# A conditional linear layer and a mixture of experts on one core: weight masks by halves on two engines, one bank for counts and ranks, an uneven last store

## The chip, the cores and the metric

The kernel runs on one core of a Trainium2 chip. The metric is device time in microseconds (us), the median of several runs; a run counts from the start of the program's execution on the core to its end. A profile is one execution of its own, with a time of its own. In it, PE is TensorE's matmuls and PEld its weight loads, DVE is VectorE, ACT is ScalarE, POOL is GpSimd, SP is SyncE. A name with a q behind it (SPq, ACTq) is that engine's queue, from which it issues transfers.

## The reference

Two layers with residuals over x of 128 batch rows x 32 tokens x 128 features, in float32. The first builds a weight matrix for every batch row from eight masked ones; the second routes every batch row to two of eight experts and adds a shared MLP.

```python
masked_w = weight * mask[None, :, :]                  # (8, 128, 128)
w_bot = einsum('bg,got->bot', cond_8, masked_w)
x = x + einsum('bnt,bot->bno', x, w_bot) + bias
...
rw = softmax(cond_8); w, sel = top_k(rw, 2)            # per batch row
w = w / w.sum(-1)                                     # and a scaling that keeps the value
out = sum over experts of dense_w[:, e] * mlp_e(x)    # gelu(x gate_e) * (x up_e), times down_e
x = x + out + mlp_shared(x)                           # all MLPs 128 -> 512 -> 128
```

## The kernel before, in words

Everything is held transposed: features on 128 partitions, the 4096 tokens along the free axis, in eight tiles of 512 (NTILE = 8, TB = 512; one tile holds 16 batch rows). The order of instructions on each engine is the order of the program text. It has three parts.

**Conditional layer, woven with the routing.** The eight weights arrive as four transfers of 128 KB, in turns on SP and ACT (L88 to L94); the mask follows the first on SP, then come two tiles of x, the bias, the shared MLP and the other six tiles. POOL makes the identity `ident` and the constant `ones` (L124 to L126). `warm_up(n)` (L130) issues n matmuls of ones by ones on PE, whose result nobody reads: four first, and six behind the transpose of the conditions, `ps_y` (L227). One float32 matmul is two records, here called passes; a transpose is one.

DVE then forms `mw`, weight times mask (L233 to L239), in four operations of two weights each, and after them `yd` (L241), which spreads `ps_y` over the eight weights. `transpose_weights` (L250) turns `mw` by eight transposes on PE, two to a bank; ACT and DVE copy the four banks in turns to `wT`. At its end it takes three steps of the routing.

`make_weights(i, half)` (L275) is one unit: 16 matmuls of 32 rows (32 passes) into four banks, which give 64 of the 128 outputs for 32 batch rows, in the order: block k outside, bank j inside. Then ACT copies banks 0 and 2 to `W`, DVE banks 1 and 3. There are eight units, 0 to 7; units 2i and 2i+1 belong to pair i of tiles. `apply_weights(t)` (L301) multiplies x by W into a bank `pz`, ACT copies it to `z`; `finish_cond(t)` (L320) transposes z back into a bank `pt`, DVE adds bias and x to give `x1`, and for tiles from 2 on POOL copies x1 to `acc`. The loop at L677 to L693 runs three units, and then, for pair i, two apply_weights, `advance(4)`, two units while there are any, and two finish_cond.

PSUM has eight banks in three pools: three g, three u, two o. `bank()` (L268) takes them by the cycle "guoguogu". A bank is taken when it is first written, and is free again after its last reader.

`routing()` (L353) is a generator. A `yield` ends a step of one to three small operations on DVE; `advance(n)` takes up to n steps, after it has issued the matmuls that earlier steps left behind (`tensor_later`). `yield ROUND` ends an advance. Step 5 asks for two matmuls: `ps_n`, how many rows each expert has, into a g bank, and `ps_p`, each row's rank in its expert, into a u bank (L372 to L375). They run at the start of the advance in pair 1. `count` (L403, step 10) reads ps_n, `slot` and `over` (L461 and L465) read ps_p.

**Experts.** Each tile gathers up to six batch rows of one expert (192 tokens): SP loads the three weights, POOL copies the rows, `Mlp` runs the matmuls, DVE adds the weighted result to `acc`. Two shared tiles run ahead of them.

**Late shared tiles.** Tiles 2 to 7 of the shared MLP. `Mlp.hidden` makes 512 columns of one of four hidden blocks (gate and up on PE, gelu on ACT, product `h` on DVE), `Mlp.down` multiplies it into `ps_out`. A `Pipeline` keeps `lag` blocks between the two. The last tile has `parts=2` (L725): its output is summed in two banks of 256 columns, first columns 0 to 255 and then the rest for every block; `finish` (L609) adds acc to each and stores the first from SP, the second from ACT.

Of the kernel before, what the change touches and what calls it, by code (L numbers as in the profile page):

```python
# [10 lines left out]
F32 = mybir.dt.float32  # L11
# [3 lines left out]
ALU = mybir.AluOpType  # L15
# [7 lines left out]
S = 6  # L23
S2 = 4
# [6 lines left out]
def kernel(  # L31
# [37 lines left out]
    const = ctx.enter_context(tc.tile_pool(name="const", bufs=1))  # L69
    small = ctx.enter_context(tc.tile_pool(name="small", bufs=1))  # L70
# [14 lines left out]
    cond_sb = const.tile([B, G], F32, name="cond_sb")  # L85
    nc.scalar.dma_start(out=cond_sb, in_=cond)
    mask_sb = const.tile([P, P], F32, name="mask_sb")
    GQ = 2  # L88
    w0_sb = []
    for q in range(G // GQ):  # L90
        wq = const.tile([P, GQ, P], F32, name=f"w0_{q}", tag=f"w0_{q}")
        engine = nc.scalar if q % 2 else nc.sync
        engine.dma_start(out=wq, in_=w0T[:, ts(q, GQ), :])
        w0_sb.append(wq)  # L94
        if q == 0:
            nc.sync.dma_start(out=mask_sb, in_=maskT)
    x_sb = []

    def load_x(t):
# [18 lines left out]
    shared = load_mlp(const, sgate, sup, sdown, "s")  # L118
    for t in range(EARLY, NTILE):
        load_x(t)  # L120


    ident = const.tile([P, P], F32, name="ident")
    make_identity(nc, ident)  # L124
    ones = const.tile([P, P], F32, name="ones")
    nc.gpsimd.memset(ones, 1.0)  # L126

    warm = ps_u.tile([P, TB], F32, name="warm", tag="u")

    def warm_up(n):  # L130
        for _ in range(n):
            nc.tensor.matmul(warm[:, 0:P], ones, ones, start=True, stop=True)  # L132

    warm_up(4)
    table = small.tile([P, 1], F32, name="table")
    nc.scalar.activation(table, ones[:, 0:1], AF.Exp)

# [3 lines left out]
        out=own,  # L141
        in_=ones[:, 0:R],
# [7 lines left out]
        out=own,  # L150
        in_=own,
# [9 lines left out]
        out=before,  # L161
        in_=ones,
# [30 lines left out]
    before_h = const.tile([P, P], BF16, name="before_h")  # L193
# [15 lines left out]
    own4 = const.tile([P, OQ], F32, name="own4")  # L209
# [16 lines left out]
    ps_y = ps_o.tile([P, TB], F32, name="ps_y", tag="acc")  # L226
    nc.tensor.transpose(  # L227
        ps_y[:, 0:B], cond_rep.rearrange("b r g -> b (r g)"), ident
    )
    warm_up(6)  # L230

    mw = const.tile([P, P, G], F32, name="mw")
    for q in range(G // GQ):  # L233
        nc.vector.tensor_tensor(
            mw[:, :, ts(q, GQ)].rearrange("p o g -> p g o"),
            w0_sb[q],
            mask_sb.unsqueeze(1).to_broadcast([P, GQ, P]),
            ALU.mult,
        )  # L239
    yd = const.tile([P, B, OQ], F32, name="yd")  # L240
    nc.vector.tensor_tensor(  # L241
        yd,
        ps_y[:, 0:B].unsqueeze(2).to_broadcast([P, B, OQ]),
        own4.unsqueeze(1).to_broadcast([P, B, OQ]),
        ALU.mult,
    )
    wT = const.tile([P, NQ, P], F32, name="wT")
    QB = TB // P

    def transpose_weights():  # L250
        TQ = QB // 2
        for i in range(NQ // TQ):
            pool, tag = (ps_u, "u") if i % 2 else (ps_g, "g")
            pt = pool.tile([P, TQ * P], F32, name="pt", tag=tag)
            for k in range(TQ):
                q = i * TQ + k
                nc.tensor.transpose(  # L257
                    pt[:, ts(k, P)],
                    mw[:, ts(q, OB), :].rearrange("p o g -> p (o g)"),
                    ident,  # L260
                )
# [11 lines left out]
    NB = TB // (QB * OQ)  # L273

    def make_weights(i, half):  # L275

# [76 lines left out]
    def routing():  # L353
# [92 lines left out]
        for k, n, i in ((0, NE, 0), (1, NE2, NE)):  # L446
# [12 lines left out]

        slot = small.tile([P, E], F32, name="slot")  # L460
        nc.vector.scalar_tensor_tensor(  # L461
            slot, tile0[:, 0, :], float(S), ps_p[:, 0:E], ALU.mult, ALU.add
        )
        over = small.tile([P, E], F32, name="over")
        nc.vector.scalar_tensor_tensor(  # L465
            over, tiles[:, 0, :], float(S), ps_p[:, 0:E], ALU.mult, ALU.is_le
        )
        yield
        end = small.tile([P, E], F32, name="end")
# [56 lines left out]
    class Mlp:  # L526


        def __init__(self, n, x_in, weights, finish, parts=1):
            self.n, self.x_in, self.finish, self.parts = n, x_in, finish, parts  # L530
# [26 lines left out]
            nc.vector.tensor_tensor(h[:, 0:n], ge[:, 0:n], pu[:, 0:n], ALU.mult)  # L557
            return h

        def down(self, group, h):  # L560
            if self.ps is None:
                self.ps = [
                    ps_o.tile([P, TB], F32, name="ps_out", tag="acc")
                    for _ in range(self.parts)
                ]
            w = self.n // self.parts
            for part, ps in enumerate(self.ps):
                for i, c in enumerate(group):
                    self.product(
                        ps[:, 0:w],  # L570
                        self.wd[:, c, :],
                        h[:, i * self.n + part * w : i * self.n + (part + 1) * w],
                        start=(c == 0),
                        stop=(c == NCH - 1),
                    )
                if group[-1] == NCH - 1:
                    self.finish(ps, part)

    class Pipeline:

# [22 lines left out]

    pipe = Pipeline(h_pool)

    def shared_tile(t, parts=1):
        w = TB // parts

        def finish(ps, part):  # L609
            cols = slice(t * TB + part * w, t * TB + (part + 1) * w)  # L610
            if t < EARLY:
                nc.vector.tensor_tensor(acc[:, cols], ps[:, 0:w], x1[:, cols], ALU.add)
            else:
                o = o_pool.tile([P, w], F32, name="o", tag="o")
                nc.vector.tensor_tensor(o, ps[:, 0:w], acc[:, cols], ALU.add)  # L615
                queue = nc.scalar if part % 2 else nc.sync
                queue.dma_start(out=outT[:, cols], in_=o)

        return Mlp(TB, x1[:, ts(t, TB)], shared, finish, parts)

    def tokens(i, pairs, engine):
        _, values = nc.values_load_multi_w_load_instructions(
# [46 lines left out]
    def weights():  # L669
        unit = units.pop(0)  # L670
        next(unit)
        next(unit)
# [6 lines left out]
    for i in range(LAST + 1):  # L679
        for t in range(PAIR):  # L680
            apply_weights(i * PAIR + t)
        advance(4)

        for _ in units[0:2]:
            weights()
        if i == LAST:
            pipe.run(first, slice(1, 2))
        for t in range(PAIR):
            finish_cond(i * PAIR + t)
        if i == LAST - 1:  # L690
            first = shared_tile(0)
            pipe.run(first, slice(0, 1))
            advance(2)  # L693
# [34 lines left out]

    with tc.If(n_used > SURE, preferred_fallthrough_block=False) as more_tiles:
# [64 lines left out]
```

## Time and profile before

| What | us |
|---|---|
| median of three runs (289.8 to 290.52) | 290.5 |
| the profiled execution, its own time | 289.53 |
| its span, first to last instruction | 287.8 |
| PE busy in the span | 281.1 (98%) |
| DVE busy | 166.6 (58%) |
| ACT busy | 78.9 (27%) |
| POOL busy | 48.4 (17%) |
| landing of the first weights, issued at 0.82 | 2.2 later |
| landing of the mask, issued at 1.26 | 3.0 later |
| the mask products on DVE, four | 4.32 to 6.36 |
| first expert matmul | 50.17 |
| last instruction of an engine (DVE, the last add) | ends at 283.86 |

The busy times are sums over the whole span. In the chain that ended last, each line is a piece: when it began, how long it lasted, and what ran, with x and the number of instructions. In the timeline, each line is a group of like instructions: start, time, engine, line of the code, operation, what it writes and reads with shapes, how many, and in brackets how long the engine had been idle before and for what it had waited. Matmuls overlap in PE's pipeline, so the spacing of their starts tells their cost, not the time of one.

### The profile page before, as it was taken

Reading aid. Unit: us, or ns where it says so; the run is one execution under the profiler, and the core shown is the slowest. Engines: PE = TensorE matmul, PEld = TensorE weight load, DVE = VectorE, ACT = ScalarE, POOL = GpSimd, SP = SyncE. Lnnn points to the kernel's source line nnn. Section 1 sums busy time; section 2 is a strip of 40 time slices with the busy share of each in tenths; the row PEclk is TensorE's granted clock in tenths of the full one; section 3 lists DMA queues with packets and bytes.
Section 4 is the critical chain, followed back from the end, with each engine's and each line's share of the span. In section 5 each row is a group of like instructions: output and inputs, shape, how many; then the busy total and the mean of one; then the engine's idle time right before and its main releaser. Section 6 shows DMA issues by size and latency. Waiting matters only on the chain.

```text
span 287.8 us, 12876 instructions
## 1 busy us (share of the span) xinstructions
PE 281.1 (98%) x5098; PEld 209.0 (73%) x5098; DVE 166.6 (58%) x472; ACT 78.9 (27%) x149; POOL 48.4 (17%) x288
## 2 busy tenths in 40 slices
PE   7999999999999999999999999999999999999993
PEld 7987644687888878878888899999997444444442
DVE  4879783366656666756666666566666333233232
ACT  4655312222222222222222222222222221222220
POOL 3002203122222212222222221312200000000000
PEclk9999999999999999999999999999999999999999
DMA  6800077276658667687667776787710200100001
GB/s 205 281 5 3 0 191 249 77 216 192 204 188 249 205 205 213 198 247 219 197 205 224 211 210 204 206 241 206 218 43 2 74 36 0 39 36 8 28 36 46
DMA packets 41058, 41.86 MB, mean 145 GB/s; under 512 B 2848, under 2 KB 27296, under 8 KB 40992
## 3 DMA queue, kind: packets, MB, share of 16 engines
q1 hardware_dynamic: 40416, 40.58, 46.3%
q8 instruction: 42, 0.69, 1.0%
q10 hardware_dynamic: 576, 0.40, 0.4%
q14 instruction: 24, 0.20, 0.2%
HBM read 38.87 MB, written 2.10 MB: 142 GB/s over the span
## 4 chain that ended last, share of the span: by engine, by line
PE 97%; DVE 1%; POOL 0%; issue 0%; POOLq 0%
PE pg L542 30%; PE ps_out L542 29%; PE pu L542 29%; PE w L282 3%; PE pz L307 3%; PE warm L132 2%; PE pt L324 1%; PE pt L257 0%; DVE o L615 0%; DVE W L296 0%; PE ps_w L347 0%; PE ps_y L227 0%; POOL ident masks.py:199 0%; POOL ident masks.py:197 0%; POOL ones L126 0%
## 5 line engine op out<-in xcount | busy, mean ns | idle before, releaser
L557 DVE TENSOR_TENSOR h<-ge,pu 128x384 f32<-128x384 f32 (+1 forms) x117 | 69.4, 593 | 76.6 <-PE pu L542 74.8
L555 ACT ACTIVATE ge<-pg 128x384 f32<-128x384 f32 (+1 forms) x117 | 61.5, 526 | 189.0 <-PE pg L542 185.5
L655 DVE SCALAR_TENSOR_TENSOR acc<-ps_out,slot_w,acc 128x32 f32 x260 | 65.3, 251 | 30.5 <-DVE h L557 19.5
L542 PE MATMUL pg<-xg,wg 128*32 128x192 f32 (+1 forms) x1440 | 75.7, 320 | 0.0
L542 PE MATMUL ps_out<-h,wd 128*32 128x192 f32 (+1 forms) x1440 | 75.7, 320 | 0.0
L542 PE MATMUL pu<-xg,wu 128*32 128x192 f32 (+1 forms) x1440 | 75.7, 320 | 0.0
L650 POOL COPY xg<-x 128x32 f32 x260 | 42.0, 209 | 132.3 <-PE pu L542 120.1
L542 PEld LDWEIGHTS pg<-xg,wg 128*32 128x32 f32 x1440 | 51.6, 110 | 9.1 <-issue 1.7
L542 PEld LDWEIGHTS pu<-xg,wu 128*32 128x32 f32 x1440 | 52.0, 110 | 7.5
L542 PEld LDWEIGHTS ps_out<-h,wd 128*32 128x32 f32 x1440 | 51.4, 110 | 8.3 <-DVE acc L655 0.8
L542 PE MATMUL pg<-x,swg 128*128 128x512 f32 x64 | 33.0, 597 | 0.0
L542 PE MATMUL pu<-x,swu 128*128 128x512 f32 x64 | 32.7, 592 | 0.0
L542 PE MATMUL ps_out<-h,swd 128*128 128x512 f32 (+1 forms) x72 | 32.5, 546 | 0.0
L542 PEld LDWEIGHTS ps_out<-h,swd 128*128 128x128 f32 x72 | 13.6, 190 | 14.5 <-issue 13.2
L542 PEld LDWEIGHTS pu<-x,swu 128*128 128x128 f32 x64 | 12.2, 190 | 15.3 <-issue 14.8
L542 PEld LDWEIGHTS pg<-x,swg 128*128 128x128 f32 x64 | 11.8, 190 | 12.8 <-issue 12.4
L296 DVE COPY W<-w 128x512 f32<-128x512 f32 x16 | 10.0, 685 | 2.2 <-PE w L282 2.1
L282 PE MATMUL w<-yd,wT 32*128 32x128 f32 x256 | 9.9, 281 | 0.6 <-DVE W L296 0.6
L282 PEld LDWEIGHTS w<-yd,wT 32*128 32x128 f32 x256 | 8.9, 186 | 1.5 <-DVE W L296 0.8
L298 ACT COPY W<-w 128x512 f32<-128x512 f32 x16 | 8.4, 596 | 3.8 <-PE w L282 3.8
L329 POOL COPY acc<-x 128x512 f32<-128x512 f32 x6 | 3.7, 614 | 28.5 <-DVE x L325 28.4
L307 PE MATMUL pz<-W,xin 128*32 128x128 f32 x256 | 7.8, 274 | 0.1
(94 smaller groups left out, 68.9 us busy)
## 6 DMA issues: line engine op xcount, KB each, us to landing
wg<-in_gate_dram SPq DMA_DIRECT2D x45, 256.0 KB, 3.6
wu<-in_up_dram SPq DMA_DIRECT2D x45, 256.0 KB, 3.9
wd<-in_down_dram SPq DMA_DIRECT2D x45, 256.0 KB, 3.5
xin<-in_xT_dram SPq DMA_DIRECT2D x8, 256.0 KB, 5.6
out_dram<-o SPq DMA_DIRECT2D x5, 256.0 KB, 2.0
out_dram<-acc SPq DMA_DIRECT2D x2, 256.0 KB, 2.3
w<-in_w0T_dram SPq DMA_DIRECT2D x2, 128.0 KB, 2.8
w<-in_w0T_dram ACTq DMA_DIRECT2D x2, 128.0 KB, 3.3
```

The source lines that it names most:

```text
L132: nc.tensor.matmul(warm[:, 0:P], ones, ones, start=True, stop=True)
L282: nc.tensor.matmul(banks[j][:, ts(k, NB * OQ)], wT[rows, q0 + k, :], yd[rows, ts(i, NB), :].rearrange("p b o -> p (b o)"), start=True, sto ...
L296: nc.vector.tensor_copy(dst, src)
L298: nc.scalar.copy(dst, src)
L307: nc.tensor.matmul(pz[j * N : (j + 1) * N, ts(k, P)], x_sb[t][:, ts(b, N)], W[:, t * BT + b, :], start=True, stop=True,)
L324: nc.tensor.transpose(pt[:, ts(k, P)], z[:, ts(k, P)], ident)
L329: nc.gpsimd.tensor_copy(acc[:, ts(t, TB)], x1[:, ts(t, TB)])
L542: nc.tensor.matmul(out[rows], w[:, rows], x, **flags)
L555: nc.scalar.activation(ge[:, 0:n], pg[:, 0:n], AF.Gelu_apprx_tanh)
L557: nc.vector.tensor_tensor(h[:, 0:n], ge[:, 0:n], pu[:, 0:n], ALU.mult)
L650: nc.gpsimd.tensor_copy(xg[:, ts(j, N)], x1[:, bass.ds(v, N)])
L655: nc.vector.scalar_tensor_tensor(a, ps[:, ts(j, N)], slot_w[:, slot0 + j : slot0 + j + 1], a, ALU.mult, ALU.add,)
```

## The change

Six edits, all outside the experts' part. The weights come in two transfers of 256 KB, one on SP and one on ACT, and the mask is SP's second transfer. `ones` is made first on DVE, ahead of the identity. The warm matmuls are six and three instead of four and six. The mask product is cut by halves of the 128 outputs; in each half DVE makes the first four weights and POOL the other four. `yd` is spread in two parts: 32 batch rows ahead of the products, the other 96 at the end of `transpose_weights`, where three routing steps stood before. Counts and ranks share one bank of the cycle, which is copied to `np_sb` before it is used; the routing's steps are taken as 5 in pair 0, and 4, 1 and 1 in pair 1 (one behind each unit), where there were 3, 4 and 4. The last tile is summed in parts of 384 and 128 columns, and for its last two blocks all of the first part comes before the second.

```diff
-    GQ = 2
+    GQ = G // 2
     w0_sb = []
-    for q in range(G // GQ):
+    for q, engine in enumerate((nc.sync, nc.scalar)):
         wq = const.tile([P, GQ, P], F32, name=f"w0_{q}", tag=f"w0_{q}")
-        engine = nc.scalar if q % 2 else nc.sync
         engine.dma_start(out=wq, in_=w0T[:, ts(q, GQ), :])
         w0_sb.append(wq)
-        if q == 0:
-            nc.sync.dma_start(out=mask_sb, in_=maskT)
+    nc.sync.dma_start(out=mask_sb, in_=maskT)
...
+    ones = const.tile([P, P], F32, name="ones")
+    nc.vector.memset(ones, 1.0)
     ident = const.tile([P, P], F32, name="ident")
     make_identity(nc, ident)
-    ones = const.tile([P, P], F32, name="ones")
-    nc.gpsimd.memset(ones, 1.0)
...
-    warm_up(4)
+    warm_up(6)
...
-    warm_up(6)
+    warm_up(3)
+    yd = const.tile([P, B, OQ], F32, name="yd")
+
+    def spread_cond(b0, n):
+        nc.vector.tensor_tensor(
+            yd[:, b0 : b0 + n, :],
+            ps_y[:, b0 : b0 + n].unsqueeze(2).to_broadcast([P, n, OQ]),
+            own4.unsqueeze(1).to_broadcast([P, n, OQ]),
+            ALU.mult,
+        )
+
+    QB = TB // P
+    NB = TB // (QB * OQ)
+    spread_cond(0, NB)
...
     mw = const.tile([P, P, G], F32, name="mw")
-    for q in range(G // GQ):
-        nc.vector.tensor_tensor(
-            mw[:, :, ts(q, GQ)].rearrange("p o g -> p g o"),
-            w0_sb[q],
-            mask_sb.unsqueeze(1).to_broadcast([P, GQ, P]),
-            ALU.mult,
-        )
-    yd = const.tile([P, B, OQ], F32, name="yd")
-    nc.vector.tensor_tensor(
-        yd,
-        ps_y[:, 0:B].unsqueeze(2).to_broadcast([P, B, OQ]),
-        own4.unsqueeze(1).to_broadcast([P, B, OQ]),
-        ALU.mult,
-    )
+    OH = QB * OB
+    for half in range(P // OH):
+        for q, engine in enumerate((nc.vector, nc.gpsimd)):
+            engine.tensor_tensor(
+                mw[:, ts(half, OH), ts(q, GQ)].rearrange("p o g -> p g o"),
+                w0_sb[q][:, :, ts(half, OH)],
+                mask_sb[:, ts(half, OH)].unsqueeze(1).to_broadcast([P, GQ, OH]),
+                ALU.mult,
+            )
     wT = const.tile([P, NQ, P], F32, name="wT")
...
             copy(wT[:, ts(i, TQ), :].rearrange("p q t -> p (q t)"), pt)
-        advance(3)
+        spread_cond(NB, B - NB)
...
-        ps_n = ps_g.tile([P, TB], F32, name="ps_n", tag="g")
-        ps_p = ps_u.tile([P, TB], F32, name="ps_p", tag="u")
+        ps_n = bank("ps_n")
         tensor_later(ps_n[:, 0:E], ones_h, chosen, start=True, stop=True)
-        tensor_later(ps_p[:, 0:E], before_h, chosen, start=True, stop=True)
+        tensor_later(ps_n[:, E : 2 * E], before_h, chosen, start=True, stop=True)
...
         yield ROUND
+        np_sb = small.tile([P, 2 * E], F32, name="np_sb")
+        nc.vector.tensor_copy(np_sb, ps_n[:, 0 : 2 * E])
+        of_expert, so_far = np_sb[:, 0:E], np_sb[:, E : 2 * E]
...
-        nc.vector.tensor_scalar(count, ps_n[:, 0:E], -(S2 + 0.5), None, ALU.add)
+        nc.vector.tensor_scalar(count, of_expert, -(S2 + 0.5), None, ALU.add)
...
-            w = self.n // self.parts
-            for part, ps in enumerate(self.ps):
+            for cols, ps in list(zip(self.parts, self.ps))[parts]:
                 for i, c in enumerate(group):
...
-                queue = nc.scalar if part % 2 else nc.sync
+                queue = nc.scalar if part.start else nc.sync
...
-        advance(4)
+        advance(5 if i == 0 else 4)
 
         for _ in units[0:2]:
             weights()
+            if i == 1:
+                advance(1)
...
         pipe.lag = 2
-        pipe.run(shared_tile(NTILE - 1, parts=2))
-        pipe.drain()
+        pipe.run(shared_tile(NTILE - 1, (TB - P, P)))
+        for part in range(2):
+            for mlp, group, h in pipe.pending:
+                mlp.down(group, h, slice(part, part + 1))
```

More of the change, by code (lines that the diff above doesn't have):

```diff
@@ L229 @@
     )
-    warm_up(6)
-    mw = const.tile([P, P, G], F32, name="mw")
-    for q in range(G // GQ):
+    warm_up(3)
+    yd = const.tile([P, B, OQ], F32, name="yd")
+    def spread_cond(b0, n):
         nc.vector.tensor_tensor(
-            mw[:, :, ts(q, GQ)].rearrange("p o g -> p g o"),
-            w0_sb[q],
-            mask_sb.unsqueeze(1).to_broadcast([P, GQ, P]),
+            yd[:, b0 : b0 + n, :],
+            ps_y[:, b0 : b0 + n].unsqueeze(2).to_broadcast([P, n, OQ]),
+            own4.unsqueeze(1).to_broadcast([P, n, OQ]),
             ALU.mult,
         )
-    yd = const.tile([P, B, OQ], F32, name="yd")
-    nc.vector.tensor_tensor(
-        yd,
-        ps_y[:, 0:B].unsqueeze(2).to_broadcast([P, B, OQ]),
-        own4.unsqueeze(1).to_broadcast([P, B, OQ]),
-        ALU.mult,
-    )
+    QB = TB // P
+    NB = TB // (QB * OQ)
+    spread_cond(0, NB)
+    mw = const.tile([P, P, G], F32, name="mw")
+    OH = QB * OB
[7 more added lines that the diff above has]
+            )
     wT = const.tile([P, NQ, P], F32, name="wT")
-    QB = TB // P
     def transpose_weights():
@@ L271, in bank @@
         return pool.tile([P, TB], F32, name=name, tag=tag)
-    NB = TB // (QB * OQ)
     def make_weights(i, half):
@@ L461, in routing @@
         nc.vector.scalar_tensor_tensor(
-            slot, tile0[:, 0, :], float(S), ps_p[:, 0:E], ALU.mult, ALU.add
+            slot, tile0[:, 0, :], float(S), so_far, ALU.mult, ALU.add
         )
@@ L465, in routing @@
         nc.vector.scalar_tensor_tensor(
-            over, tiles[:, 0, :], float(S), ps_p[:, 0:E], ALU.mult, ALU.is_le
+            over, tiles[:, 0, :], float(S), so_far, ALU.mult, ALU.is_le
         )
@@ L526, with __init__ @@
     class Mlp:
-        def __init__(self, n, x_in, weights, finish, parts=1):
-            self.n, self.x_in, self.finish, self.parts = n, x_in, finish, parts
+        def __init__(self, n, x_in, weights, finish, widths=None):
+            self.n, self.x_in, self.finish = n, x_in, finish
+            self.parts = [slice(0, n)]
+            if widths:
+                ends = list(itertools.accumulate(widths))
+                self.parts = [slice(e - w, e) for w, e in zip(widths, ends)]
             self.wg, self.wu, self.wd = weights
@@ L558, in hidden, with down @@
             return h
-        def down(self, group, h):
+        def down(self, group, h, parts=slice(None)):
             if self.ps is None:
                 self.ps = [
-                    ps_o.tile([P, TB], F32, name="ps_out", tag="acc")
-                    for _ in range(self.parts)
-                ]
-            w = self.n // self.parts
-            for part, ps in enumerate(self.ps):
+                    ps_o.tile([P, TB], F32, name="ps_out", tag="acc") for _ in self.parts
+                ]
+            for cols, ps in list(zip(self.parts, self.ps))[parts]:
                 for i, c in enumerate(group):
                     self.product(
-                        ps[:, 0:w],
+                        ps[:, 0 : cols.stop - cols.start],
                         self.wd[:, c, :],
-                        h[:, i * self.n + part * w : i * self.n + (part + 1) * w],
+                        h[:, i * self.n + cols.start : i * self.n + cols.stop],
                         start=(c == 0),
@@ L576, in down @@
                 if group[-1] == NCH - 1:
-                    self.finish(ps, part)
+                    self.finish(ps, cols)
     class Pipeline:
@@ L604, with shared_tile @@
     pipe = Pipeline(h_pool)
-    def shared_tile(t, parts=1):
-        w = TB // parts
+    def shared_tile(t, widths=None):
         def finish(ps, part):
-            cols = slice(t * TB + part * w, t * TB + (part + 1) * w)
+            w = part.stop - part.start
+            cols = slice(t * TB + part.start, t * TB + part.stop)
             if t < EARLY:
@@ L615, in finish @@
                 nc.vector.tensor_tensor(o, ps[:, 0:w], acc[:, cols], ALU.add)
-                queue = nc.scalar if part % 2 else nc.sync
+                queue = nc.scalar if part.start else nc.sync
                 queue.dma_start(out=outT[:, cols], in_=o)
-        return Mlp(TB, x1[:, ts(t, TB)], shared, finish, parts)
+        return Mlp(TB, x1[:, ts(t, TB)], shared, finish, widths)
     def tokens(i, pairs, engine):
```

## The prediction, made before the changed kernel was run

> **What bounds the kernel now.** I read the shares of the chain of work that ended last first, then that chain in order of time from 0 to 24 us, then the timeline of the stretches that the diff touches.
>
> ```profile
> PE 97%; DVE 1%; POOL 0%; issue 0%; POOLq 0%
> ```
>
> TensorE (PE) sets the end. From 22 us to 283 us the chain is PE behind PE without a hole, so an edit counts only if it starts that stream earlier, takes a hole out of it before 22 us, or shortens what follows its last matmul.
>
> ```profile
> 1.39 0.16 POOL ones L126
> 1.54 0.04 issue
> 1.59 2.08 PE warm L132 x8
> 3.67 0.38 PE ps_y L227
> 4.04 2.56 PE warm L132 x12
> 6.61 0.93 PE pt L257 x8
> 7.54 3.73 PE w L282 x96
> 11.27 0.09 issue
> 11.36 1.95 PE pz L307 x64
> 13.31 2.03 PE w L282 x64
> ...
> 18.38 1.18 PE w L282 x32
> 19.56 0.68 DVE W L296
> 20.25 0.04 issue
> 20.29 1.49 PE w L282 x28
> 21.78 1.13 PE pt L324 x8
> ```
>
> A unit of make_weights is 32 passes. Two of them take 2.03 us undisturbed (13.31). Units 5 and 6, from 18.38 to 21.78, take 3.40 for the same 64 passes: 1.37 us are lost. The first three units take 3.73 where 3.05 would do: they wait for copies out of PSUM.
>
> Why 1.37: count the banks by the ring "guoguogu". Three g, three u and two o banks exist; from 18.2 on ps_n holds a g (until L403 at 24.18) and ps_p a u (until L465 at 35.3). Unit 5 takes o g u o, unit 6 g u g u. The third bank of unit 6 is unit 5's g, free after VectorE's (DVE's) first copy at 20.23; the fourth is unit 5's u, free after ScalarE's (ACT's) second copy near 20.6. The trace fits: four passes of unit 6 run at once, the other 28 start at 20.29 and need 1.49 instead of 0.9.
>
> **The change, part by part.**
>
> *Start of the clock.* ones is made on DVE instead of behind the identity on POOL. PE now starts at 1.59; DVE's first instruction in the trace waits for POOL until 2.10, so its earliest start is unseen, but POOL and the DMA queues begin at 0.81. I take PE at 1.05, half a microsecond earlier. It gives nothing directly: twelve warm passes take 2.08 + 4 x 0.214 (2.56/12) = 2.93 and end at 4.0, so ps_y moves from 3.67 to 4.0. cond_rep is ready at 3.52, so the transpose of cond is 0.35 later. Six warm passes follow, to 5.7.
>
> *Masking.* Now: four DVE products of 256 elements, 2.04 us together from 4.32 (when the mask lands), 0.47 apart, 0.64 long. Transposes from 6.42, first unit at 7.47, DVE's first copy W at 8.78. After: per half one DVE and one POOL product of 256 elements. POOL has no such row. Nearest: its copy of 128x512 took 0.614, of 128x32 0.209; a product of 256 reads as much as the 512 copy, so I take 0.65. Bounds: 0.40 (a one-input copy of 256, interpolated) and 0.92 (0.61 times 0.64/0.425, what DVE's masked product costs over its plain 256-element add).
>
> Do the two run side by side? The timeline speaks:
>
> ```profile
> 23.67 1.27 POOL L329 COPY acc<-x 128x512 f32<-128x512 f32 x2 [20.00 <-DVE x L325]
> ...
> 24.45 0.68 DVE L407 SCALAR_TENSOR_TENSOR full<-slot_iota,count 128x176 f32<-128x176 f32 x1
> ...
> 34.59 1.27 POOL L329 COPY acc<-x 128x512 f32<-128x512 f32 x2 [5.35 <-DVE x L325]
> ...
> 35.34 0.54 DVE L470 TENSOR_TENSOR end<-tiles,tile 128x8 f32<-128x8 f32 x1
> ```
>
> An 8-element product takes 0.54 where its neighbours take 0.17, and ends at 35.88, when POOL's copy ends (35.86). `full` ends 0.19 after POOL's end at 24.94. The Trainium skill, "SBUF — State Buffer", section "SBUF: two separate sides", gives the rule, which speaks against this change: a DVE operation with two SBUF inputs and a GpSimd operation that reads SBUF exclude each other for a whole instruction. Both rows are cases of it; POOL's product waiting for DVE is not shown here. By rule and row the four products queue up: mask at 4.35 (unmoved: 320 KB on SP and 260 KB on ACT are the bytes that had come by then before), POOL 0.65, DVE 0.5, POOL 0.65, DVE 0.5, end at 6.65 against 6.36 now. Side by side they would end at 5.8.
>
> *What follows.* In the queued case transposes 0-3 run at 5.7, 4-7 at 6.7-7.2; PE is in order, so the first unit starts near 7.25 instead of 7.47. DVE has behind its last product: wT copy (0.43), wT copy after the last transpose (to 7.75), then the second spread_cond of 384 elements (0.683 x 3/4, about 0.55, to 8.3), where today three routing steps end at 8.86. Unit 0 is done at 8.5, so the first copy W moves from 8.78 to 8.6. From there to pz (11.36) today's order holds, because unit 2 waits for unit 0's banks and pz for unit 1's copies. Gain 0.2. Side by side, PE's warm passes hold the transposes until 5.7; while each pass still takes 0.214 they end near 7.0, the copies start at 8.3, gain 0.5. I take 0.3. The first spread_cond (128 elements, 0.25) lies under POOL's first product. ps_y now holds its o bank to 8.3; unit 1's second bank needs it about then: zero. It costs 0.25 if that cover is gone.
>
> *DMA.* Two 256 KB loads replace four of 128 KB; SP and ACT issue one fewer each (0.42 and 0.46), x and bias move up, the mask goes behind a load twice as large. Its wait is the risk: it lands 3.0 us after issue today; bound 4.1 to 4.7, so -0.2 to +0.4.
>
> *One bank.* ps_n and ps_p share a bank of the ring, read by one more DVE copy of 16 elements (about 0.16, as L403) between units 5 and 6. The ring moves by one: unit 5 takes g u o g, unit 6 u g u o. Still short: unit 6's second bank is a g, two are unit 5's and one is ps_n's. It waits for ACT's first copy of unit 5, starting 19.5, ending 20.09; then 30 passes need 0.95. Unit 6 ends at 21.1 instead of 21.78. Gain 0.7; 1.37 if the wait goes altogether, 0 if DVE gets in the way. DVE's steps move up: rw to we (seven operations, 1.3 us) now stand before unit 5's copies; from 18.19 that is 19.5, where the copies begin today (19.55, after 0.72 idle). np_sb, count and `full` (0.34 without POOL beside it) go around unit 6, where DVE idled 0.82. After them wait unit 6's copies, x1 of tiles 2 and 3, then unit 7's copies at about 26.2 - 0.3 (today 25.96). pz of the last pair needs those by 28.64 - 1.0: they end at 27.2. It holds by 0.4 us.
>
> Later routing comes two steps, slot_token one group earlier. PE does not wait for weights or xg, so zero.
>
> *Tail.*
>
> ```profile
> 280.64 2.75 PE L542 MATMUL ps_out<-h,swd 128*128 128x256 f32 x12
> ...
> 283.00 0.86 DVE L615 TENSOR_TENSOR o<-ps_out,acc 128x256 f32<-128x256 f32 x2 [1.40 <-PE ps_out L542]
> 283.45 0.33 SPq L617 DMA_DIRECT2D out_dram<-o  x1
> 283.89 0.35 ACTq L617 DMA_DIRECT2D out_dram<-o  x1
> ```
>
> The last passes end at T = 283.39 (280.80 + 12 x 0.2155). After: the 384-column part ends 4 x 0.107 = 0.43 before T, its add (0.56, between 0.425 for 256 and 0.69 for 512) ends at T + 0.16, the 128-column add (0.29) at T + 0.45. Today T + 0.47. So only the last store's size is left, 64 KB instead of 128 KB (2.3 to land). Sizes do not order the landings: 256 KB took 2.0, 4 KB took 2.4. Between +0.3 and -0.1 (eight 128-column passes at a transpose's 0.12 instead of 0.107); I take 0.1.
>
> *Sum:* 0.3 + 0.7 + 0.1 = 1.1. The profiled execution took 289.53 (span 287.8 and 1.73 around it), so its like would be 288.4; that execution lies 1.0 under the median 290.5 of the runs shown, so the forecast is 290.5 - 1.1 = **289.4**.
>
> **The rivals.**
>
> *Products side by side, and the bank wait gone entirely* (20%): 0.5 + 1.3 + 0.2 = 2.0, 288.5. For it: two engines, half the work each. Against: the two DVE rows, and the ring.
>
> *The bank wait is replaced* (15%): DVE, with 1.3 us of routing before unit 5's copies and three operations around unit 6, comes late, and PE stands at unit 6 or at pz as long as before. Margins are 0.05 and 0.4 us. Left: 0.3 to 0.4, 290.2.
>
> *PE stays at its slow pace longer; slower* (11%). Warm passes start 0.214 apart up to 6.2, transposes of the same width 0.12 apart after 6.4: PE doubled its pace there, though the granted clock reads 1.00 throughout. The skill, "TensorE: Matmul & The Clock Gate", Part 1, says why: the clock is halved until a window of about 3.4 us has been busy, and the windows do not start with the kernel. Today PE is full from 1.59 to 6.42. After, it is empty from about 6.2 to 6.7 and perhaps at 5.7, and two warm passes fewer are issued. If a window is missed, the next ends one window later (estimate 6.4 + 3.4 = 9.8). Transposes 4-7 cost 0.4 more, and units and pz run at half pace: from 7.7 to 9.8 half of 2.1 is lost, 1.5 together, and time is 290.9. It ends slower than before once the slow pace outlasts 9.0. Two windows would be 292.5. Against: PE is still over 80% busy in that stretch.
>
> **How the numbers follow.** 54% for 289.4 (own range 288.9 to 290.0), 20% for 288.5, 15% for 290.2, 11% for 290.9 or more. About 0.3%, 0.87 us, is what can be told from no change: faster is under 289.63, slower over 291.37. Faster: 0.68 of the first case, all of the second, 0.1 of the third: 0.58. Slower: over half of the last: 0.07. Range: 288.3 to 290.9, which leaves out half of the last case and the edge of the second.
>
> **What would show it.** PE's first pass near 1.05; four mask products one after another, DVE's lengthened to over 1 us where it waits for POOL (side by side: none over 0.7); the mask's landing; first copy W near 8.6, pz near 11.1; in the chain units 5 and 6 at 2.7 instead of 3.40, behind an ACT copy W; pz of the last pair without a hole; PE's pass spacing before and after 6.4. I am wrong if POOL's product takes over 1.2 us (each 0.1 more costs 0.2), if DVE cannot start before 1.5, or if the pace doubles late.

## The result, and the profile after

The changed kernel takes 288.93 us, the median of 22 runs (288.45 to 290.34), against 290.5 for the kernel before on the same chip (22 runs, 289.04 to 291.54). The ratio is 0.9953, with a 95% interval from 0.994 to 0.9966: about 1.4 us less. The profiled execution took 288.74 (span 287.0), where that of before took 289.53 (span 287.8). These two differ by 0.8, less than the medians do, so I account for the 0.8 first and leave the rest to the experiments.

PE still has 97% of the chain that ended last. The chain after in order of time, for the stretches shown of before (start, us, what ran):

```profile
0.81 3.09 DMA cond_sb<-in_cond_dram
...
7.72 3.66 PE w L286 x93
...
11.46 1.95 PE pz L311 x64
13.42 1.31 PE w L286 x34
14.73 0.13 issue
14.86 1.17 PE w L286 x30
...
19.07 1.26 PE w L286 x31
20.33 0.57 ACT W L302
...
20.95 1.17 PE w L286 x30
```

Four things stand in it. The chain begins with the transfer of the conditions, so PE's earlier start (1.13 instead of 1.59) buys nothing there. pz, the end of the front, begins at 11.46, a tenth later than before (11.36). Units 3 and 4, from 13.42 to 16.02, take 2.60, with a hole in them, where before they took 2.03. Units 5 and 6, from 19.07 to 22.11, take 3.04 instead of 3.40, behind an ACT copy W, as forecast. Until here, then, the changed kernel is behind: 0.1 in the front, 0.57 in units 3 and 4, and 0.36 won back. PE's last matmul ends at 283.58, against 283.39 before. The changed kernel is faster only after that.

The masking, in the timeline of after:

```profile
4.78 1.68 POOL L248 TENSOR_TENSOR mw<-w,mask_sb 128x256 f32<-128x256 f32 x2 [1.38 <-DMA w<-in_w0T_dram]
...
4.99 1.95 DVE L248 TENSOR_TENSOR mw<-w,mask_sb 128x256 f32<-128x256 f32 x2
```

Taken apart, the four products are POOL 4.78 to 5.51, DVE 4.99 to 5.99, POOL 5.47 to 6.46, DVE 5.83 to 6.94: 0.73, then 1.0, 1.0 and 1.1, where each has the wait for the other engine inside it. What ends POOL's idle time (1.38) is the landing of the weights, not of the mask. DVE's first product stands behind the first part of `yd`, which waits for `ps_y` until 4.78. The landings of the front, in us after the issue (the last number), before:

```profile
w<-in_w0T_dram SPq DMA_DIRECT2D x2, 128.0 KB, 2.8
w<-in_w0T_dram ACTq DMA_DIRECT2D x2, 128.0 KB, 3.3
mask_sb<-in_maskT_dram SPq DMA_DIRECT2D x1, 64.0 KB, 3.0
cond_sb<-in_cond_dram ACTq DMA_DIRECT2D x1, 4.0 KB, 2.4
```

And after:

```profile
w<-in_w0T_dram SPq DMA_DIRECT2D x1, 256.0 KB, 2.9
w<-in_w0T_dram ACTq DMA_DIRECT2D x1, 256.0 KB, 3.5
mask_sb<-in_maskT_dram SPq DMA_DIRECT2D x1, 64.0 KB, 3.1
cond_sb<-in_cond_dram ACTq DMA_DIRECT2D x1, 4.0 KB, 3.1
```

The mask lands as before, at 4.33. ACT's weights land at 4.71, and the 4 KB of conditions at 3.90 instead of 3.25.

The tail in the timeline of after:

```profile
280.82 2.77 PE L552 MATMUL ps_out<-h,swd 128*128 128x384 f32 x12
283.18 0.75 DVE L622 TENSOR_TENSOR o<-ps_out,acc 128x384 f32<-128x384 f32 x2 [1.40 <-PE ps_out L552]
```

The add of the last 128 columns ends at 283.93, 0.35 after PE, where before the last add ended 0.47 after. The stores are issued at 283.76 and 283.96 and both land 2.2 later. From PE's end to the last landing it is 2.59, against 2.83.

What is left is behind the last landing. SP's wait for the two stores is 2.2 us in total before, with 2.0 the longer of the two, and after 1.0, with 0.9. The line of the code that does it, with the number of its instructions and the first and last start in us, before and after:

```profile
L790 SPq EVENT_SEMAPHORE  x10: 17/28/28, 286.0 to 287.8; - x10
```

```profile
L801 SPq EVENT_SEMAPHORE  x10: 17/28/28, 284.4 to 287.0; - x10
```

The columns between are the durations in ns. The trace shows that the program counts its transfers on eight semaphores in turn, and that at its end SP waits for the eight one after another, in a fixed order. Before, the last two stores have the first two of them: SP stands 2.0 us at the first wait, and the other six, with a gap of 0.37 among them, come behind the last landing. So all ten instructions lie between 286.0 and 287.8, and from SP's seeing the last landing (286.22) to the end of the span it is 1.61. The changed kernel has two loads fewer. That moves its last two stores to the seventh and eighth semaphore; the six other waits are done from 284.4 on, while the stores are still under way, and from the last landing seen (286.17) to the end it is 0.87. Nothing in the six edits aims at this: it is a side effect of four weight loads becoming two.

The sum for the profiled pair: front -0.10, units 3 and 4 -0.57, units 5 and 6 +0.36, +0.12 over the rest of PE's stream, PE's end to the last landing +0.24, closing waits +0.74. That is 0.79.

### The profile page after: what moved, and what is told of

Read it like the earlier page. It is cut to its first block, busy times and chain, and to the rows that moved or that the text cites. A ratio compares the mean times of both kernels' runs of the same rounds, so it can differ in the third digit from the quotient of the medians.

```text
span 287.0 us, 12878 instructions
## 1 busy us (share of the span) xinstructions
PE 281.3 (98%) x5096; PEld 211.5 (74%) x5096; DVE 166.4 (58%) x473; ACT 79.0 (28%) x149; POOL 49.9 (17%) x289
## 4 chain that ended last, share of the span: by engine, by line
PE 97%; DMA 1%; issue 0%; DVE 0%; ACT 0%
PE pg L552 30%; PE ps_out L552 29%; PE pu L552 29%; PE w L286 3%; PE pz L311 3%; PE pt L328 1%; DMA cond_sb<-in_cond_dram 1%; PE pt L263 1%; PE warm L130 0%; ACT W L302 0%; PE ps_w L351 0%; PE ps_y L225 0%; DVE o L622 0%; DVE cond_rep L213 0%; PE ps_n L351 0%
## 5 line engine op out<-in xcount | busy, mean ns | idle before, releaser
L662 DVE SCALAR_TENSOR_TENSOR acc<-ps_out,slot_w,acc 128x32 f32 x260 | 65.2, 251 | 30.0 <-DVE h L567 19.5
L552 PE MATMUL ps_out<-h,wd 128*32 128x192 f32 (+1 forms) x1440 | 74.2, 320 | 0.0
L552 PE MATMUL pg<-xg,wg 128*32 128x192 f32 (+1 forms) x1440 | 74.0, 320 | 0.0
L552 PE MATMUL pu<-xg,wu 128*32 128x192 f32 (+1 forms) x1440 | 73.9, 320 | 0.0
L552 PEld LDWEIGHTS pg<-xg,wg 128*32 128x32 f32 x1440 | 50.8, 110 | 8.0 <-issue 1.7
L552 PEld LDWEIGHTS pu<-xg,wu 128*32 128x32 f32 x1440 | 51.0, 110 | 6.4
L552 PE MATMUL ps_out<-h,swd 128*128 128x512 f32 (+2 forms) x72 | 32.5, 546 | 0.0
L300 DVE COPY W<-w 128x512 f32<-128x512 f32 x16 | 10.1, 684 | 1.4 <-PE w L286 1.4
L286 PE MATMUL w<-yd,wT 32*128 32x128 f32 x256 | 10.1, 284 | 0.6 <-ACT W L302 0.5
```

The source lines that it names most:

```text
L286: nc.tensor.matmul(banks[j][:, ts(k, NB * OQ)], wT[rows, q0 + k, :], yd[rows, ts(i, NB), :].rearrange("p b o -> p (b o)"), start=True, sto ...
L300: nc.vector.tensor_copy(dst, src)
L552: nc.tensor.matmul(out[rows], w[:, rows], x, **flags)
L662: nc.vector.scalar_tensor_tensor(a, ps[:, ts(j, N)], slot_w[:, slot0 + j : slot0 + j + 1], a, ALU.mult, ALU.add,)
```

## The experiments

The theory after the traces (A): the order of the closing waits gives about 0.7 us and the one bank the rest, the front nothing. The rivals: the uneven tail (B) or the early ones (C) carry the gain. All kernels were timed in turn with the kernel before, whose medians in the three groups were 289.95, 290.28 and 289.87 us; the ratios are against these.

**The order of the closing waits.** e1 is the changed kernel with two small loads more, which put its last two stores back on the first two semaphores. e2 is the kernel before with six of them, which put its last two on the seventh and eighth.

```diff
+    for i in range(2):                      # 6 in e2
+        extra = const.tile([P, 1], F32, name=f"extra{i}", tag=f"extra{i}")
+        nc.sync.dma_start(out=extra, in_=bias)
     late = shared_tile(EARLY)
```

> The changed kernel with two more transfers of 0.5 KB (the bias, read by nobody), issued by SP once its last expert weights are asked for, near 210 us. They move the two last stores from the seventh and eighth of SP's eight closing waits to the first and second. Theory A (the order of the closing waits): in the profiles SP's last wait on a landing ends at 286.22 before and 286.17 after, but the span ends at 287.8 and 287.0; before, seven more waits still stand behind the first. Then this run loses 0.8 us against the changed kernel: ratio to the kernel before 0.998, closing part (last landing to end of span) 1.6 us instead of 0.8. Theory B (the smaller last store) and theory C (the gain is at the front): nothing changes, ratio 0.995.

> The kernel before with six more transfers of 0.5 KB at the same place, which put its two last stores at the seventh and eighth closing wait, as in the changed kernel. Nothing else is changed. Theory A: faster by 0.8 us, ratio 0.997. Theories B and C: ratio 1.000 (six issues on SP, which waits there for weight buffers, cost nothing).

The closing waits of SP in e1, and then in e2:

```profile
L804 SPq EVENT_SEMAPHORE  x10: 17/28/28, 285.6 to 287.4; - x10
```

```profile
L793 SPq EVENT_SEMAPHORE  x10: 17/28/28, 285.7 to 288.2; - x10
```

e1: 289.47 us, ratio 0.9979 [0.9963, 0.9994], as A expects: two loads of 512 bytes that nobody waits for take back half of the gain (the interval just touches that of the changed kernel). Its closing waits are those of before (1.9 us for the two stores, 1.7 at the first), and from the last landing seen (285.86) to the end it is 1.60. e2: 289.76, 0.999 [0.9978, 1.0002]. The closing part did shrink to 0.87 in its profile (last landing seen at 287.40), but the time fell by 0.3 us and not by 0.75, and the interval holds 1. By e2's time alone, no gain is shown.

**The tail alone, and the early ones alone.** e3 is the kernel before with only the parts of 384 and 128 columns; e4 is the kernel before with only `ones` on DVE and six warm passes in both places.

```diff
-        pipe.run(shared_tile(NTILE - 1, parts=2))          # e3
-        pipe.drain()
+        pipe.run(shared_tile(NTILE - 1, (TB - P, P)))
+        for part in range(2):
+            for mlp, group, h in pipe.pending:
+                mlp.down(group, h, slice(part, part + 1))
...
+    nc.vector.memset(ones, 1.0)                            # e4
     ident = const.tile([P, P], F32, name="ident")
     make_identity(nc, ident)
-    nc.gpsimd.memset(ones, 1.0)
-    warm_up(4)
+    warm_up(6)
```

> The kernel before with the uneven last tile alone (384 and 128 columns, all of the first part ahead for the last two blocks). The forecast's term was 0.1 us (-0.1 to 0.3): ratio 0.9997. Theory A agrees, since the stores stay at the first and second closing wait. Theory B: this part holds most of the gain, ratio 0.997.

> The kernel before with ones made first on DVE and six warm matmuls ahead of the transpose of the conditions instead of four, so that TensorE begins near 1.1 us instead of 1.59; the six behind the transpose are kept. Theory C (the pace of TensorE doubles some time after its first work, at another point in every run, and an earlier start takes the late cases away): median 0.5 us lower, ratio 0.998, and a narrower spread of the runs than the 2.5 us of the kernel before. Theory A: ratio 1.000 or, as the warm passes now end at 6.7 instead of 6.4, 0.3 us slower.

e3: 290.24, ratio 1.0002 [0.9985, 1.0019]. e4: 290.21, 1.0005 [0.9988, 1.0022]. Neither B nor C carries the gain. In profiles, too, the way from PE's end to the last landing is no shorter with the uneven tail: 2.58 to 2.94 (after, e1, e3, e5, e6, e8, e9, e10), and 2.67 to 2.90 with the even one (before, e2, e4). The +0.24 of the profiled pair lies within that spread.

**The bank.** e5 is the changed kernel once more, beside e6, the changed kernel with ps_n and ps_p in banks of their own as before, without np_sb and without the two single steps in pair 1.

```diff
-        ps_n = bank("ps_n")
+        ps_n = ps_g.tile([P, TB], F32, name="ps_n", tag="g")
+        ps_p = ps_u.tile([P, TB], F32, name="ps_p", tag="u")
...
-        np_sb = small.tile([P, 2 * E], F32, name="np_sb")
-        nc.vector.tensor_copy(np_sb, ps_n[:, 0 : 2 * E])
...
-            if i == 1:
-                advance(1)
```

> The changed kernel once more, beside the three kernels below on one chip, so that each can be set against it. Ratio 0.995 again, closing part 0.87 us.

> The changed kernel with ps_n in a g bank and ps_p in a u bank again, no np_sb, and no advance(1) behind the units of pair 1. Theory D (the bank edit gives what the traces show, units 5 and 6 in 3.04 us instead of 3.40): they go back to 3.40, 0.4 us slower than the changed kernel. Theory E (the bank edit also costs, since it moves the cycle of banks under units 3 and 4, which took 2.60 instead of 2.03): units 3 and 4 go back to 2.0 and the run is 0.2 us faster than the changed kernel. If the hole at 14.7 us has to do with what TensorE is fed with and not with banks (it stands as issue, in the kernel before with six transfers too), units 3 and 4 stay at 2.2 to 2.7.

e5: 288.91, 0.9955 [0.9935, 0.9974]. e6: 289.88, 0.9977 [0.9965, 0.9988], and units 5 and 6 are back at 3.40 us (19.82 to 23.22). In its chain the wait stands behind a DVE copy again:

```profile
21.05 0.17 DVE we L403
21.21 0.61 DVE W L300
21.83 0.04 issue
21.87 1.42 PE w L286 x28
```

So the bank is worth 0.0022, 0.64 us; the two intervals overlap, so by this pair alone it is no sharp number. e6 also keeps the changed order of the routing: `we` and six operations stand ahead of unit 5's copies, and DVE's begin 1.39 after the unit does, in before 1.24. The cleaner pair is e9, described below, beside e2: they differ in the bank and the tail only, and the ratios are 0.996 and 0.999, with intervals that do not overlap (0.0030, 0.87 us). The chain shows 0.36 to 0.47 (3.04 in after, 2.93 in e5, against 3.40).

The profiles of e5 and e6 held something else. In the chain of e5:

```profile
6.25 2.02 PE pt L263 x8
8.27 4.38 PE w L286 x95
...
12.74 1.95 PE pz L311 x64
```

pz begins at 12.74, not 11.46. The eight transposes follow each other without a hole and yet take 2.02; the groups of four passes of unit 0 stand 0.21 us apart, and only from 9.7 on 0.11, where in after they do so from the second group on. It is the rival in which PE stays at its slow pace longer: in e6 as well (pz at 12.89), in none of the other six profiles of a changed front, and in none of the six that mask as before (pz at 11.2 to 11.8).

The views show a granted clock of 1.00 here, but that is no measurement. The trace's own record of the clock begins at 9.74 in e5 and at 10.09 in e6, and a stretch without a record is shown as 1.00. In before it begins at 6.51, in after at 6.59. In all fourteen profiles it begins where PE's passes double their pace, from 4.64 (e1) to 10.09. So the doubling is the clock. Behind the last work of PE the rows do show 0.50 (in before from 286.4 on).

Both executions lie 0.8 above the medians of their kernels (289.69 and 290.70). In both, units 3 and 4 then have no hole (2.00), which gives 0.6 of the 1.3 back.

**The masking engines.** e7 has all four half products on DVE.

```diff
-        for q, engine in enumerate((nc.vector, nc.gpsimd)):
+        for q, engine in enumerate((nc.vector, nc.vector)):
```

> The changed kernel with all four mask products on DVE, in the same halves. In the changed kernel POOL and DVE took turns, 0.73 and 0.48 us each, 4.78 to 6.94. Theory F (the two engines exclude each other, so POOL's share brings nothing): four times 0.48, end 0.2 us sooner from the same landing, the first pass of the transposes for half 0 about the same; ratio to the changed kernel 0.999 to 1.000. If POOL did help, the last product ends 0.3 or more later and the run loses as much.

e7: 289.97, 0.9996 [0.9983, 1.0009], slower than the changed kernel (e5, in the same group) by 1.1 us. The expectation failed, and the profile of its front gives no reason: products from 4.93 to 6.95, pz at 11.41 (after: 11.46). But its last store landed late. Two kernels took this up. e11 is the changed kernel, products on both engines, with two writes of one column more on DVE, at the start where it idles. e12 is e7 with three such writes on POOL, so that POOL's program is as long as in the changed kernel.

```diff
+    extra = const.tile([P, 2], F32, name="extra")          # e11
+    for i in range(2):
+        nc.vector.memset(extra[:, i : i + 1], 0.0)
     ident = const.tile([P, P], F32, name="ident")
```

> The changed kernel with two 1-column writes more on DVE at its start, where it idles: POOL keeps its mask products, and DVE's program is as long as in the kernel with all products on DVE, which took 1 us more than its profile of the front explains. Theory G: where DVE's program ends within a code load, and so when the closing code is fetched, moves the landing of the last store: 289.9, ratio near 0.999, ACT's store landing 2.9 us after issue as there. Theory H: the 1 us comes from the products themselves: as the changed kernel, 0.9955, landing 2.2.

> All four mask products on DVE, and three 1-column writes on POOL behind them, so that POOL's program is as long as in the changed kernel. Theory H (the products themselves): 289.9 again, ratio near 0.9993, with the pace doubling late or the first copy late in its profile. Theory G (DVE's program length): 289.9 too, ACT's store 2.9 us after issue. POOL's program length decides: 288.9, 0.9955. If it comes out near 289.2, the run before had drawn badly among its executions.

e11: 289.6, 0.9985 [0.9975, 0.9994]. e12: 289.43, 0.9984 [0.9973, 0.9995]. With DVE's program equally long, it makes no difference which engine masks (e7's own ratio is 0.0012 higher than e12's, within the intervals); and two DVE instructions that do nothing cost 0.9 us by the ratios (0.9985 against 0.9955). The DMA view of the last microseconds has the queues (packets, MB, share of 16 engines) and the landing of each store. In after:

```profile
out_dram<-o ACTq DMA_DIRECT2D x1, 64.0 KB, 2.2
```

And in e11:

```profile
q14 instruction: 4, 0.03, 1.6%
q8 instruction: 2, 0.03, 1.5%
...
out_dram<-o ACTq DMA_DIRECT2D x1, 64.0 KB, 3.0
```

ACT's store of 64 KB lands 3.0 us after issue instead of 2.2. It is 2.9 in e7 and 3.3 in e12, and 2.2 to 2.5 in the eleven other profiles: late in just the three kernels whose DVE program is two instructions longer. The rows "instruction" are code being loaded, four blocks of 8 KB and two of 16 KB. By the trace's packets, three of the 8 KB loads start at 285.96, 285.96 and 286.26 in e11, on the tail of the store; its last 512-byte packets take 46 to 99 ns each instead of 27, and the last ends at 286.67, 2.16 after issue (1.70 in after, where the loads are spread from 284.31 to 287.03). From the last packet to the landing it is then 0.88 instead of 0.49. That the collision makes the delay, the timing of the packets argues, and for the first part only; that DVE's length decides it, the three kernels show. How the length sets the times of the loads was not tried.

**The front undone, and an earlier copy.** e9 is the kernel before with the one bank, the uneven tail and e2's six small loads: the changed kernel but for the edits of the front. e8 is the changed kernel with the copy to np_sb taken one step earlier, ahead of unit 5's copies; e10 is e9 with that.

```diff
-        yield ROUND                                        # e8, e10
         np_sb = small.tile([P, 2 * E], F32, name="np_sb")
         nc.vector.tensor_copy(np_sb, ps_n[:, 0 : 2 * E])
         of_expert, so_far = np_sb[:, 0:E], np_sb[:, E : 2 * E]
+        yield ROUND
```

> The changed kernel with the copy to np_sb one step sooner: behind we, ahead of the copies W of unit 5, instead of behind them. In the changed kernel unit 6 stops after two passes until ACT's first copy W (20.33 to 20.90) because ps_n holds the third g bank. Theory D: ps_n is free near 20.2, the stop falls away, units 5 and 6 take 2.1 to 2.4 us instead of 3.04, and DVE's copies of unit 5 begin 0.17 later. 0.5 us faster than the changed kernel, ratio to the kernel before 0.9935. If DVE's copies are what counts there, no change.

> The kernel before with the one bank and the uneven tail, and with six extra 0.5 KB loads so that its last two stores stand seventh and eighth among the closing waits, as in the changed kernel. Not in it: the early ones with six warm passes, the two larger weight loads, the masking by halves on two engines, the spread in two parts. Front is worth nothing: the same ratio as the changed kernel, 0.9955 (within 0.001). Front is worth the forecast 0.3 us: 0.9965 or more. Front costs something (its wait for the 256 KB load, POOL and DVE in turns, 1.3 us in executions where the pace doubles late): 0.9935 or less.

> The same, and the copy of counts and ranks moved ahead of unit 5's copies, as in the run before that beat both kernels (0.9938). If the front is worth nothing, 0.9938 again, with units 5 and 6 at 2.3 us. If the front costs, under 0.992, and this is the fastest version; if it gains, 0.995.

e8: 288.44, 0.9938 [0.9919, 0.9956]. The bank of the counts is free before unit 6 needs it, and ACT's copy is gone from the chain. Units 5 and 6 are one piece in the chain of e8:

```profile
18.86 0.14 PE ps_n L351 x2
19.00 2.30 PE w L286 x64
```

e9: 288.64, 0.996 [0.9947, 0.9974]. e10: 287.94 (6 runs), 0.993 [0.9907, 0.9954], units 5 and 6 at 2.02. So e9, without any edit of the front, has 0.0040 of the changed kernel's 0.0045 to 0.0047: the bank, the tail and the order of the waits carry the gain. Against e5 the front undone is 0.0005 slower, against e8 0.0008 faster: the front shows no effect, on either side. By the times alone its forecast 0.3 us can't be excluded, since each of these comparisons is good to 0.7 us at best (estimate from the two intervals). The profiles say more: where PE was at its fast pace from 7.5 us on, pz begins at 11.35 to 11.46 with the changed front (six, mean 11.39) and at 11.24 to 11.79 with the front of before (six, mean 11.46). e10 and e8 beat both kernels, e10 with the front of before.

## Why the prediction was right, and where it was not

The time (288.93, forecast 289.4) and the direction were right. The working was right for the bank; the gain as a whole is right partly by luck, since two terms that came to nothing were made up for by one that was not in the sum.

- **One bank, forecast 0.7.** Measured 0.64 (e6) and 0.87 (e9 beside e2) in time, 0.36 in the profiled pair; behind ACT's copy of unit 5, as worked out. In the chain it is half of the forecast for two reasons: the copy ended 1.83 after unit 5's start in the chain instead of 1.71, and the 30 passes behind it took 1.17 instead of 0.95. The copies began 0.8 later than the forecast put them (20.31 instead of 19.5), since unit 5 itself began later. That the wait would not go altogether, by the ring and the place of the copy, was right: e8 moves the copy and gains another 0.0017.
- **Front, forecast 0.3.** No effect shown by e9 and e10, and 0.07 on average at pz. The queueing was right: POOL, DVE, POOL, DVE in turns, as the Trainium skill has it ("SBUF — State Buffer", "SBUF: two separate sides") for a two-input DVE operation beside a GpSimd one, and POOL's product waiting for DVE's, which no row of before had shown, is shown (1.0 beside 0.73). The products took 2.16, forecast 2.3, and the four all on DVE 2.02: the second engine bought nothing. What failed is the start. The sum let the products begin with the mask, at 4.35. The mask did land at 4.33, but a half of the outputs needs all eight weights at once, and ACT's load of 256 KB landed at 4.71, 3.5 after its issue; the products began at 4.78. The trace of before had the warning: the two weight loads that the sum counts among the bytes that had come by 4.35 landed only at 5.11 and 5.29, and the products that needed them ran last. With four loads of 128 KB the products began at 3.7 to 4.3. The second miss is the conditions. Their 4 KB landed 3.0 to 3.3 after issue in the eight profiles with two weight loads and 2.4 in the six with four, so ps_y ran at 4.30, later than the 4.0 of the sum. The first part of `yd`, which the sum laid under POOL's product, waited for it and held DVE's first product until 4.99 (4.93 in e7, where DVE masks alone). So the first copy W came at 8.88, not 8.6. The early ones did move PE's first pass (1.13, forecast 1.05).
- **Tail, forecast 0.1.** Measured -0.0002 ± 0.0017 in the ratio by e3, which can't tell it from 0.1.
- **Not in the sum: the closing waits.** 0.74 in the profiled pair, 0.75 by e1 against the changed kernel (0.9979 against 0.9953), 0.3 by e2, whose interval holds no gain too. The step that failed is the one in which the two loads fewer were costed only by their issue and their landing. The trace of before had it: ten instructions of SP behind 286.0.
- **PE at its slow pace longer, 11%.** It happens, in two of eight profiled executions of a changed front, and it costs about what was worked out (pz 1.3 later; 1.5 forecast), but 0.8 in the end. It was put as a case of the kernel; it is one of the execution, and how often it comes outside the profiles is not known. The prediction read the granted clock as 1.00 throughout; the record of it begins at 6.51 in before, where the pace doubles. The Trainium skill's rule behind the rival ("TensorE: Matmul & The Clock Gate", Part 1) fits: the record begins at 9.74 in e5, near the 9.8 estimated from it, and the stretch at full clock lasts 279.9 or 283.3 us in all fourteen profiles, lengths that lie 3.4 apart.
- **Side by side (20%)** is refuted by the product rows. **The bank wait replaced (15%)** is refuted by units 5 and 6 (3.04 instead of 3.40) and by e9 beside e2.

Open are two things. Why the order of the waits shows 0.3 in time on the kernel before and 0.75 on the changed one was not found; the intervals overlap, so it may be one number. And the hole in units 3 and 4 goes with a 16 KB code load, by its size and number PE's, which began at 12.4 to 13.1 in the changed fronts and from 11.2 to 12.6 in the others. Where the load had ended 0.4 us or more before unit 3 began, the units took 2.00 to 2.03 (before, e5, e6, e10); in the other ten profiles, where it ended later, they took 2.13 to 3.00. At the fast pace that is 2.60 to 3.00 with the changed front (six profiles) and 2.00 to 2.69 with the front of before (six). That may be where a small gain of the front goes; no experiment moved the load.

## What to carry to other kernels

Read the last two microseconds of the page as closely as the bottleneck: which transfer the first of the closing waits is for, and what else is being fetched when the last store lands. In a kernel that is tuned to a few tenths, adding or dropping a load or an instruction far from the end moved the time by 0.3 to 0.9 us here, as much as the edits themselves; so an experiment that adds operations should be read by its landings and waits before its time is put down to what it tests. Before cutting work into pieces of another shape, ask which transfers the first piece now needs: cut by weights, the products before could begin with the first loads; cut by outputs, they waited for the last. A second engine beside DVE on SBUF operands is worth its row only if the trace shows the two at work together; here they took turns.

## What the runs showed of the hardware that was not expected

- Transfers are counted on eight semaphores in turn, and the closing waits come in a fixed order: 0.87 us from the last landing to the end if the last stores are on the last two (ten profiles), 1.60 to 1.61 if they are on the first two (four).
- Two idle DVE instructions at the start cost 0.9 us at the end. In the three profiles with that length the last store lands 2.9 to 3.3 us after issue instead of 2.2 to 2.5, and code loads of 8 KB meet its last packets; that these are the cause is argued, not shown.
- At the start of the kernel, a load of 256 KB on ACT's queue landed 3.4 to 3.8 us after issue (eight profiles). POOL's first product, which waits for it, started at 4.7 to 5.1 (six); with four loads of half the size DVE's first started at 3.7 to 4.3 (six). The 4 KB of conditions, issued ahead of it on the same queue, landed 3.0 to 3.3 after issue instead of 2.4.
- PE's passes doubled their pace anywhere from 4.6 to 10.1 us between executions and kernels, each time where the record of the granted clock begins; after and e5, one kernel, had it at 6.6 and at 9.7.
